# Four buffers in place of twenty for the normalised tiles of layer 0's router and scatter

## The chip, the cores and the metric

The kernel runs on one core of a Trainium2 chip. A core has five engines, each with its own queue that it works through in order: TensorE (PE in the profile; its weight loads are shown as PEld), VectorE (DVE), ScalarE (ACT), GpSimd (POOL) and SyncE (SP). Engines meet through semaphores: an instruction waits until another engine's, or a transfer's, count has been reached. The metric is device time in microseconds (us) of one execution, lower is better. Each run also shows the span from the program's first to its last instruction, and the TensorE clock that the chip granted (1.0 is full speed).

## What is computed

Four layers over x of 2 x 2048 tokens with 256 features in float32. Each layer normalises x and adds two branches to it. Only layer 0 matters here:

```python
xn = layernorm(x)                                   # 4096 tokens, 256 features
x = x + gated_linear_attention(xn) + experts(xn)    # layer 0

def experts(xn):                                    # 8 experts, the best 2 of each token
    w, idx = top_k(xn @ Wr, 2)
    comb = sum(softmax(w)[:, :, None] * one_hot(idx, 8), axis=1)
    h, g = xn @ W1[e], xn @ W3[e]                   # for each expert e
    y = (silu(h) * g) @ W2[e]
    return einsum('nec,ne->nc', y, comb)

def gated_linear_attention(x):                      # 4 heads, a state carried over the tokens
    q, k, v = x @ Wq / 8, x @ Wk, x @ Wv
    gk = log_sigmoid(x @ Wgk1 @ Wgk2 + bgk2) / 16
    S = S * exp(gk_t)[:, None] + k_t v_t^T;  o_t = q_t S      # for each token t
    return (rmsnorm(o) * g_norm_weight * silu(x @ Wg)) @ Wo
```

Layers 1 to 3 (a selective scan with a table of small experts, a retention layer, softmax attention of 16 heads with a second feed-forward branch) follow and are not touched. Layer 1 gathers rows of its tables with GpSimd's indirect DMAs, 512 of them at L805.

## The kernel before, in words

Tokens stand on the 128 partitions, so x is 32 tiles of 128 x 256, and stays in on-chip memory.

Layer 0 weaves three streams into one program: the attention of the two sequences (two chains of eight blocks of 256 tokens, the class `Attn0`) and the stream `moe`, which first routes and then runs 39 expert blocks of 256 token rows. The build then puts the woven instructions of each engine into an order of its own, by what they depend on and what it believes that they take; that order is fixed before the program runs. So an instruction of one stream can stand on a queue behind one of another.

The stream `route` does, in order:

- The routing loop: eight groups of four tiles. For each, statistics (L204 to L207), the four normalised tiles by `xnorm` (L195, on VectorE, from x, mean `mv` and scale `rs`), their transposes on TensorE (L212) and copies into `xT` (L213, ScalarE), the router's products (L68, tile `ps_e`), and the best eight of each token (L219, L220).
- Counting: which row of a buffer in HBM, `xgd`, each token takes for each of its two experts. Two matmuls count tokens (L242, L243), VectorE turns the counts into row numbers `pos` (L248 to L268).
- The scatter loop: for each of the 32 tiles, `xnorm` normalises it again, and two indirect DMAs issued by GpSimd (L273) write its 128 rows to their places in `xgd`, one for each of the two experts. The 64 scatters are declared free of order among themselves. The zero fill of `xgd` (L188, from SyncE's queue) comes before them.
- The numbers of the weight rows for each expert block (L283 to L288).

An expert block loads its weights `we` with an indirect DMA of GpSimd (L295), its 256 token rows `xg` with a DMA of SyncE (L300), transposes them on TensorE (L305), copies them on ScalarE (L306), and runs its products (L68, `ps_e`) with L315 to L317 between. The first load of `xg` waits for all 64 scatters.

An attention block projects to q, k, v and the gate (L68, `ps_g`; L388, L395, L399, L400, L403), computes the decay (L411 to L426: the scan `G`; L430 to L436: `qh`, `kh`), transposes `kh` on TensorE (L444), copies it on ScalarE (L446), makes the new states (L452 on TensorE, L461 on VectorE), then goes through seven levels of the intra-block products. A level is: the exponents E on VectorE (L476, L477), an exponential on ScalarE (L478), two products on VectorE (L481 `qt`, and L485; from the third block of a sequence on, L485 is GpSimd's), eight matmuls (L489), and two predicated copies on VectorE (L494). After the levels come the diagonal (L505 on TensorE, L510 on VectorE), the output products (L523, L527), their copy (L531), the norm (L538 to L543 `o`), transposes and the output projection (L549, L551, L68), and the addition to x (L554).

The tile `xn` is taken from a pool with a number of buffers, and both loops of `route` use the same ones in turn. A tile's L195 has to wait until the instructions that read the tile one round earlier are done: the transposes L212 in the routing loop, and the landing of both scatters in the scatter loop. The pool `wk` closes when `route` ends, and the pool of the expert blocks takes its place.

Of the kernel before, what the change touches and what calls it, by code (L numbers as in the profile page):

```python
# [14 lines left out]
F32 = mybir.dt.float32  # L15
# [8 lines left out]
P = 128  # L24
B, S, D = 2, 2048, 256
# [147 lines left out]
def route(g, tc, a, rt, wk, r, xgd):  # L173
# [17 lines left out]

    def xnorm(t):

        xn = wk.tile([P, D], F32, name="xn0", tag="xn0", bufs=20)
        nc.vector.tensor_scalar(xn, g.x[:, t, :], mv[:, t, 0:1], rs[:, t : t + 1], ALU.subtract, ALU.mult)  # L195
        return xn

# [2 lines left out]
    for n in (0, 4, 1, 5, 2, 6, 3, 7):  # L200
        t4 = slice(4 * n, 4 * n + 4)
        st = wk.tile([P, 4, 6], F32, name="st0", tag="st0", bufs=2)
        for i in range(4):
            nc.vector.bn_stats(st[:, i, :], g.x[:, 4 * n + i, :])  # L204
            nc.vector.bn_aggr(mv[:, 4 * n + i, :], st[:, i, :])
        nc.scalar.activation(rs[:, t4], mv[:, t4, 1], AF.Sqrt, bias=g.eps)
        nc.vector.reciprocal(rs[:, t4], rs[:, t4])  # L207
        xns = [xnorm(4 * n + i) for i in range(4)]
        for c in range(2):
            ps = g.psum()  # L210
            for i in range(4):
                nc.tensor.transpose(ps[:, i * P : (i + 1) * P], xns[i][:, c * P : (c + 1) * P], g.ident)  # L212
            nc.scalar.copy(g.xT[:, c, n * 512 : (n + 1) * 512], ps)  # L213
        ps = g.psum2()
        for i in range(4):
            mm(nc, ps[:, i * 8 : (i + 1) * 8],
               [(g.xT[:, k, (4 * n + i) * P : (4 * n + i + 1) * P], wr[:, k, :]) for k in range(2)])
        for i in range(4):
            nc.vector.max(top[:, 4 * n + i, :], ps[:, i * 8 : (i + 1) * 8])  # L219
            nc.vector.max_index(idx[:, 4 * n + i, :], top[:, 4 * n + i, :], ps[:, i * 8 : (i + 1) * 8])  # L220
        yield
# [48 lines left out]
    for t in [16 * b + n for n in range(NT // 2) for b in range(2)]:  # L270
        xn = xnorm(t)
        for j in range(2):
            ins = nc.gpsimd.indirect_dma_start(xgd, bass.IndirectOffsetOnAxis(ap=r.pos[:, j, t : t + 1], axis=0),  # L273
                                               xn, None)
            if t or j:
                tc.declare_no_dep(ins.ins, group="deal", reason="no two tokens share a row")
            tc.add_to_no_dep_group("deal", ins.ins)
        yield
        yield
# [1461 lines left out]
```

## Time and profile before

| what | us |
|---|---|
| median of 3 runs | 4375.13 |
| lowest and highest of them | 4360.28, 4397.19 |
| the profiled execution | 4351.19 |
| its span | 4349.4 |
| TensorE busy, share of the span | 3883.6, 89% |
| VectorE, ScalarE, GpSimd busy | 2536.0, 1980.0, 1302.8 |
| mean granted clock | 0.939 |

The stages, from the starts of their instructions: routing to 90 us, scatters (L273) 90.7 to 185.9 us, attention and experts to some 1200 us, then layer 1 to about 2385 us, and layers 2 and 3.

The additions of attention blocks to x (L554) start at 202, 261, 319, 377, 437, 500, 573 and so on to 1193 us. The transposes of the expert blocks (L305) start at 194, 253, 306, 368, 426, 461, 486 us for the first seven, with some 20 us from one to the next after that.

How the views are read. The page's first part gives the busy time of each engine, its second part the span in 40 slices of 109 us with the busy share in tenths. The waits name who waited for whom, with the total, the number and the longest of these waits; "remote" stands where a wait on a semaphore was ended by nothing that the profile shows, and "issue" where an engine was idle with nothing to wait for. In a timeline a row has the start, the duration, the engine, the line, the operation and the tiles that it writes and reads, and in square brackets the idle time ahead of it and what ended it. SPq and POOLq are the queues of those engines.

### The profile page before, as it was taken

Reading aid. Unit: us, or ns where it says so; the run is one execution under the profiler, and the core shown is the slowest. Engines: PE = TensorE matmul, PEld = TensorE weight load, DVE = VectorE, ACT = ScalarE, POOL = GpSimd, SP = SyncE. Lnnn points to the kernel's source line nnn. Section 1 sums busy time; section 2 is a strip of 40 time slices with the busy share of each in tenths; the row PEclk is TensorE's granted clock in tenths of the full one; section 3 lists DMA queues with packets and bytes.
Section 4 is the critical chain, followed back from the end, with each engine's and each line's share of the span. In section 5 each row is a group of like instructions: output and inputs, shape, how many; then the busy total and the mean of one; then the engine's idle time right before and its main releaser. Section 6 shows DMA issues by size and latency. Waiting matters only on the chain.

```text
span 4349.4 us, 58929 instructions
## 1 busy us (share of the span) xinstructions
PE 3883.6 (89%) x21524; PEld 2313.5 (53%) x21524; DVE 2536.0 (58%) x6438; ACT 1980.0 (46%) x3819; POOL 1302.8 (30%) x1307
## 2 busy tenths in 40 slices
PE   6388988999968898888885999999999999999999
PEld 5266666766745455455553777777433333333332
DVE  6254444454468898788888434434866655666560
ACT  3144343443345455445442332322555565566556
POOL 1402222222256665455556111112311111111201
PEclk7687999999989999999997999999999999999999
DMA  4200122222245665665568000000000000000000
GB/s 176 93 32 32 64 79 79 75 77 70 99 137 162 187 207 181 178 182 174 179 187 243 5 1 1 1 1 18 13 7 9 6 4 14 14 11 9 4 2 26
DMA packets 110947, 330.24 MB, mean 76 GB/s; under 512 B 30689, under 2 KB 63218, under 8 KB 104258
## 3 DMA queue, kind: packets, MB, share of 16 engines
q0 software_dynamic: 52720, 264.15, 19.6%
q1 hardware_dynamic: 55266, 59.22, 4.2%
q8 instruction: 170, 2.79, 0.3%
q10 hardware_dynamic: 2672, 3.10, 0.2%
q14 instruction: 119, 0.97, 0.1%
HBM read 286.69 MB, written 33.03 MB: 74 GB/s over the span
## 4 chain that ended last, share of the span: by engine, by line
PE 49%; DVE 4%; issue 2%; ACT 2%; POOL 1%; DMA 1%; another core or an unknown queue 1%; DVEq 0%; POOLq 0%; ACTq 0%
PE ps_e L1370 12%; PE ps_v L1433 6%; PE ps_a L68 6%; PE ps_f L68 6%; PE ps_m L68 4%; PE ps_c L68 3%; PE ps_k L68 2%; PE ps_m L1375 2%; PE ps_o L1059 1%; PE ps_m L1384 1%; PE ps_s L1370 1%; PE ps_h L839 1%; PE ps_s L1375 1%; DMA G<-in_tab_in,ind 1%
## 5 line engine op out<-in xcount | busy, mean ns | idle before, releaser
L1401 DVE TENSOR_REDUCE mp<-ps_m 128x1 f32<-128x512 f32 (+3 forms) x1120 | 628.1, 605 | 425.8 <-PE ps_e L1370 246.1
L1390 ACT ACTIVATE pt<-ps_e 128x512 f32<-128x512 f32 (+3 forms) x1120 | 537.2, 531 | 423.4 <-PE ps_e L1370 394.9
L1370 PE MATMUL ps_e<-qT,kT 32*128 32x512 f32 (+3 forms) x2240 | 627.8, 579 | 8.8 <-ACT pt L1390 8.8
L1375 PE MATMUL ps_m<-kT,qT 32*128 32x512 f32 (+3 forms) x2240 | 561.5, 576 | 1.1 <-DVE mp L1401 1.1
L1370 PEld LDWEIGHTS ps_e<-qT,kT 32*128 32x128 f32 x2240 | 211.0, 184 | 326.5 <-issue 116.6
L805 POOL DMA_INDIRECT G<-in_tab_in,ind x256 | 269.8, 1054 | 300.6 <-DVE ind L792 134.5
L1433 PE MATMUL ps_v<-pt,vals 128*32 128x512 f32 (+3 forms) x2560 | 307.5, 543 | 1.3 <-POOL pt L1394 0.6
L1394 POOL TENSOR_SCALAR_AFFINE_SELECT pt<-pt 128x256 f32<-128x256 f32 x256 | 104.4, 409 | 670.7 <-ACT pt L1390 670.4
L805 POOL DMA_INDIRECT G<-in_tab_out,ind x256 | 267.5, 1045 | 87.5 <-issue 58.1
L68 PE MATMUL ps_e<-xgT,we 128*128 128x256 f32 x936 | 241.6, 404 | 27.0 <-ACT xgT L306 17.2
L68 PE MATMUL ps_k<-wk,xt 128*128 128x512 f32 x512 | 263.1, 626 | 2.5 <-DVE ix L782 2.3
L68 PE MATMUL ps_f<-hb,l_b 128*128 128x512 f32 x1024 | 253.5, 400 | 0.0
L1050 DVE SCALAR_TENSOR_TENSOR hb<-ps_f,hb 128x512 fp32r<-128x512 f32 x128 | 86.7, 683 | 254.8 <-ACT hb L1049 253.5
L68 PEld LDWEIGHTS ps_e<-xgT,we 128*128 128x128 f32 x936 | 177.3, 198 | 70.6 <-ACT xgT L306 22.8
L68 PEld LDWEIGHTS ps_f<-hb,l_b 128*128 128x128 f32 x1024 | 190.1, 188 | 45.4 <-issue 7.7
L834 DVE CUSTOM_DVE_ANT_0 scr<-hid,G,gate 128x512 f32<-128x512 f32 x256 | 199.1, 778 | 19.9 <-ACT hid L821 7.3
L1375 PEld LDWEIGHTS ps_m<-kT,qT 32*128 32x128 f32 x2240 | 180.9, 184 | 25.6 <-issue 21.6
L494 DVE COPY_PREDICATED AT<-lm,ps_g 128x256 f32<-128x256 uint8 x224 | 104.8, 520 | 144.6 <-PE ps_g L489 141.3
L815 DVE CUSTOM_DVE_ANT_0 scr<-xn,G,gate 128x256 f32<-128x256 f32 x256 | 144.6, 565 | 45.3 <-DMA G<-in_tab_in,ind 42.1
L817 DVE SCALAR_TENSOR_TENSOR hid<-G,lin,hid 128x512 f32<-128x512 f32 x224 | 166.8, 745 | 2.4 <-DVE ix L782 0.4
L489 PE MATMUL ps_g<-qt,E 64*128 64x64 f32 x1792 | 138.7, 295 | 32.6 <-DVE E L485 23.9
L1049 ACT ACTIVATE hb<-ps_f 128x512 fp32r<-128x512 f32 x128 | 76.5, 597 | 200.5 <-PE ps_f L68 200.4
(426 smaller groups left out, 7667.6 us busy)
## 6 DMA issues: line engine op xcount, KB each, us to landing
xgd<-zero SPq DMA_DIRECT2D x13, 768.0 KB, 11.9
xg<-xgd SPq DMA_DIRECT2D x39, 256.0 KB, 2.9
yd<-ye SPq DMA_DIRECT2D x39, 256.0 KB, 3.1
G<-in_tab_in,ind POOLq DMA_INDIRECT x256
G<-in_tab_out,ind POOLq DMA_INDIRECT x256
kT<-qk SPq DMA_DIRECT2D x256, 16.0 KB, 1.8
out<-x SPq DMA_DIRECT2D x7, 512.0 KB, 3.3
x<-in_x ACTq DMA_DIRECT2D x4, 512.0 KB, 9.2
```

The source lines that it names most:

```text
L68: nc.tensor.matmul(out, lhsT, rhs, start=(i == 0), stop=(i == n - 1))
L489: nc.tensor.matmul(two[r][:, n * 64 : (n + 1) * 64], E[r * 64 : (r + 1) * 64, n * P : (n + 1) * P], qt[r * 64 : (r + 1) * 64, n * 64 : (n ...
L494: nc.vector.copy_predicated(AT[:, r].rearrange("p e (n t m) -> p e n t m", t=2, m=m)[:, :, :, 1, :], lm[:, li * 64 : (li + 1) * 64].unsque ...
L805: nc.gpsimd.indirect_dma_start(G, None, a[tab], bass.IndirectOffsetOnAxis(ap=k.ind[:, h, j : j + 1], axis=0))
L815: nc.vector.tensor_tensor_reduce(scr[:, 0:D], k.xn[:, j, :], G[:, 0:D], k.gate[:, h, j : j + 1], 0.0, ALU.mult, ALU.add, lin[:, h : h + 1])
L817: nc.vector.scalar_tensor_tensor(hs, G[:, D:768], lin[:, h : h + 1], hid if h == 0 else hs, ALU.mult, ALU.add)
L834: nc.vector.tensor_tensor_reduce(scr, hs, G[:, 0:512], k.gate[:, h, j : j + 1], 0.0, ALU.mult, ALU.add, lout[:, h : h + 1])
L1370: nc.tensor.matmul(te[i // step][:, i % step, c0:512], ge.kT[row(j), kt * P : (kt + 1) * P], ge.qT[row(j), qb * 512 + c0 : (qb + 1) * 512] ...
L1375: nc.tensor.matmul(tm[i // step][:, i % step, 0:w], gm.qT[row(j), qi * P : (qi + 1) * P], gm.kT[row(j), ch * 512 : ch * 512 + w], start=Tr ...
L1390: nc.scalar.activation(pt[:, o : o + step, c0:512], te[i // step][:, :, c0:512], AF.Exp, scale=0.25)
L1401: nc.vector.tensor_reduce(gm.mp[:, qi, j : j + step, ch], tm[i // step][:, :, 0:w], AX.X, ALU.max, negate=True)
L1433: nc.tensor.matmul(av[row(j), c0:512], vals[:, kt, at + 17 * j : at + 17 * j + 32], pts[j][:, c0:512], start=first, stop=last)
```

## The change

One number: the normalised tiles `xn` get four buffers in place of twenty.

```diff
     def xnorm(t):
 
-        xn = wk.tile([P, D], F32, name="xn0", tag="xn0", bufs=20)
+        xn = wk.tile([P, D], F32, name="xn0", tag="xn0", bufs=4)
         nc.vector.tensor_scalar(xn, g.x[:, t, :], mv[:, t, 0:1], rs[:, t : t + 1], ALU.subtract, ALU.mult)
         return xn
```

In the routing loop a group of four tiles now takes the buffers of the group before it. In the scatter loop a tile takes the buffer of the tile four places earlier, so that its L195 on VectorE waits for that tile's two scatters to land; before, it was the tile twenty places earlier. As the build orders by dependences, the instructions of the first part of layer 0 stand in another order on each engine than before. On TensorE's queue the first expert's transposes stand behind 290 matmuls of the attention blocks in place of 228; those of the second to sixth block behind 352, 420, 548, 608 and 736 in place of 352, 480, 608, 736 and 804; from the seventh (behind 856) on they stand at the same places. SyncE's order is the same.

## The prediction, made before the changed kernel was run

> **What bounds the kernel now.** I began with the page. TensorE is busy for 89% of the span and carries 49% of the chain of waits, so time is lost for good only where TensorE stands idle early. The slices show where: the second one (109 to 217 us) is the emptiest of the first half, 3 tenths on TensorE and 2 on VectorE. That is where GpSimd scatters (L273). The busy times by stretch sharpen it (columns: stretch, its length, then PE, PEld, DVE, ACT and POOL busy with their counts, granted clock, DMA share, GB/s):
>
> ```profile
> 104.00:127.00 23.00, 3.79 (x32) 3.52 (x32) 10.48 (x22) 5.20 (x7) 17.51 (x19) 0.50 0.27 97
> 127.00:151.00 24.00, 0.00 (x0) 0.00 (x0) 0.00 (x0) 0.60 (x1) 18.21 (x20) 0.50 0.29 104
> 151.00:170.00 19.00, 1.95 (x12) 1.55 (x14) 4.00 (x9) 1.48 (x3) 14.46 (x15) 0.50 0.29 104
> ...
> 218.00:486.00 268.00, 225.65 (x1316) 167.31 (x1314) 137.78 (x298) 108.68 (x229) 44.76 (x42) 0.83 0.10 33
> ```
>
> From 104 to 170 TensorE works 5.7 of 66 us, at a granted clock of 0.50, while GpSimd issues without a pause. So I asked the waits of VectorE, then those of ScalarE, between 85 and 195 us (columns: who for whom, us in total, times, longest), and VectorE's timeline:
>
> ```profile
> DVE AT L510 <- remote: 29.1, 2, 24.8
> DVE St L461 <- remote: 16.3, 1, 16.3
> DVE xn L195 <- DMA xgd<-xn,pos: 9.3, 6, 2.1
> ```
>
> ```profile
> ACT ks L446 <- issue: 40.9, 1, 40.9
> ```
>
> ```profile
> 107.20 0.41 DVE L195 TENSOR_SCALAR xn<-x,mv,rs 128x256 f32<-128x256 f32 x1 [1.42 <-DMA xgd<-xn,pos]
> 109.72 0.41 DVE L195 TENSOR_SCALAR xn<-x,mv,rs 128x256 f32<-128x256 f32 x1 [2.11 <-DMA xgd<-xn,pos]
> ...
> 151.72 0.72 DVE L510 COPY_PREDICATED AT<-lm,ps_g 128x512 f32<-128x512 uint8 x1 [24.78 <-remote]
> ```
>
> "Remote" means that nothing in the profile ended the wait. "Issue" is ScalarE idle with nothing to wait for. All three long ones (L510, L461, and L446 on ScalarE) read results of TensorE, whose rows say it was done: the matmuls L505 that L510 reads start at 118.34 and end at 120.39, and L510 starts 31 us later. Over the whole span VectorE has such waits of several us only here and in layer 1 (L778, 66.7 us in 13 waits), where GpSimd gathers by the same kind of DMA. So I read them as results of TensorE that become visible late while GpSimd issues indirect DMAs one behind the other; in the first 27 us of the scatters it did not happen. Last, GpSimd's own timeline: 62 scatters at 1.27 us each (0.96 busy, 0.30 between) from 90.70 to 169.72, then
>
> ```profile
> 168.76 0.96 POOL L273 DMA_INDIRECT xgd<-xn,pos  x1 [0.30 <-issue]
> 179.70 1.61 POOL L273 DMA_INDIRECT xgd<-xn,pos  x1 [9.98 <-DVE xn L195]
> ```
>
> because the last two tiles (179.03) stand on VectorE behind the stretch that waits for TensorE.
>
> **The change part by part.** No instruction is removed. Of the 32 tiles of the scatter loop, the last 12 waited for scatters before (a buffer of twenty back); now all but the first four do. In the routing loop each group of four tiles waits for the transposes of the group before.
>
> *Routing loop.* Seven groups get a wait. A group costs 8 matmuls of 1.04 us together, then four L195 of some 0.33 us from start to start, 1.4 us, which TensorE could stand idle for: seven times that is 10 us at most. But the router's and the first block's matmuls lie between the groups (31.1, 38.0, 44.0, 49.8, 67.4 us on TensorE's timeline), and TensorE afterwards waits 5.24 us for VectorE at L444 in any case. In the new order the counting matmuls L242 stand ahead of eight level matmuls and the next block's four projections, worth 2 us. I take 0, with -2 to +5 for the range.
>
> *The buffer cycle.* A scatter lands 2.5 us after its start: L195 at 109.72 was freed by the scatter of 107.21, and the one at 112.24 by that of 109.74. A tile's two scatters free its buffer 1.27 + 2.5 = 3.8 us after its first began; L195 takes 0.4. Four tiles last GpSimd 4 x 2.54 = 10.2 us. With VectorE at hand the cycle closes with 10.2 - 4.2 = 6 us to spare, so four buffers alone cost nothing. GpSimd stands only where VectorE has more than about 9 us of other work between two L195. And VectorE can no longer run ahead: it moves at 2.54 us a tile, and L400, L403, L411 and the copies L494 behind an L195 wait with it, then TensorE's next level (L489) for E and qt. That is hidden as long as VectorE has room: from 104 to 190 us it is busy for 26 of 86 us, the L195 among them. The zero-fill DMAs and the load of xg on SP's queue are not moved; xg still waits for the last scatter.
>
> *Gaps in the new order.* Between the 20th and 21st tile 24 instructions stand on VectorE, from L494 of the sixth level to the next block's E. The same piece in an undisturbed block runs from 230.43 to 242.4: 12 us, against a supply of 8.9 us (four tiles less the 1.2 us already spent), so a pause of 3.6 us. Between the 23rd and the 24th lie some 9 us (247.6 to 251.6 in the undisturbed block, and the 5.1 us wait before), against three tiles' supply of 7.6: 2 us. Together 6 us.
>
> *The sum.* The scatters' issue needs 79.0 + 2.5 = 81.5 us without pauses, 87.5 with: it ends at 90.7 + 87.5 = 178, where it ended at 185.9. Landing 2.5, the load of xg 6.2 (187.80 to 194.00), transposes and copy 1.8: the first expert could start at 189. The chain: VectorE reaches L543 of the first block near 168 (it was 186.3), L554 follows 7.9 us later (253.13 to 261.01 in the next block) at 176 (it was 202.4), and the first expert's products come 15.3 us after L554 (202.39 to 217.65), in both orders behind the second block's gate projection: 191 against 217.65. From there the order differs (experts two to six stand earlier) up to the seventh expert, which begins at 486 and is in the same place in both; TensorE is 84% busy in between and its instructions are the same, so I take what is won to stay. Gain 26 us with TensorE's results prompt. With them late, one or two waits last until GpSimd runs dry and some 6 us longer (GpSimd ended at 169.72, L461 got its result at 176.31): 6 to 12 us back. I take 18 us, nearer the undisturbed end, since GpSimd's pauses are just what lets such a wait end. The end of the gain: without any pause the first expert cannot start before 90.7 + 81.5 + 2.5 + 6.2 + 1.8 = 183, so 35 us.
>
> The profiled execution took 4351.19 (span 4349.4), so 4333 for it. The median of the runs lies 24 us above it (4375.13), so **4357**.
>
> Here a rule speaks against the change. The Trainium skill, SBUF — State Buffer, section "Who interferes with whom", has it that a DMA never contends with a compute engine. By it the late results would not come from the scatters, and holding these back would win nothing. The rows above disagree: 48 us of such waits on VectorE in 60 us of scatters, none in the 300 us behind them.
>
> **Rivals.** *Nothing is won.* GpSimd's queue already waits for the scatter eight back (22 short waits, 6.7 us), which is four tiles, so the limit is there already; and if the late results come from something else than the unbroken stream, VectorE loses the same 48 us. For it: L461 got its result 5 us late (L452 ended at 171.1, it started at 176.31) when GpSimd already stood. Time 4375, within 5 us.
>
> *Slower, by lockstep.* VectorE must wait for TensorE before a tile, GpSimd runs dry, and VectorE then waits for scatters: the two stand in turn. The new order has six places where work that reads TensorE's or ScalarE's results stands between tiles (before the 4th, 12th, 16th, 21st, 24th and 27th). Ten us of pause at each is 60 us: the issue ends at 232, the first expert starts at 232 + 10.5 = 243, 25 us late: 4400. It decides from 217.65 - 183 = 35 us of pauses on; a loss of 1% (44 us) needs 79 us, with results late by 10 us and more nearly everywhere. Against it: before 118 us nothing was late, under the same stream.
>
> *Much faster.* The plain runs lie between 9 and 46 us above the profiled one. If it is this stall that is longer in them, the change takes it away too: 18 + 24 to 18 + 46, so 42 to 64 us, around 4322.
>
> **How the numbers follow.** My forecast (a gain of 5 to 35 us, so 4340 to 4370) gets 46%, nothing won 18%, lockstep 18%, of which 10 beyond 1%, much faster 18%. A measurement of this kernel tells about 1% (44 us) from no change. So faster by more than that 18%, within it 46 + 18 + 8 = 72%, slower 10%. The range goes from the middle of the much faster case, 4322, to 20 us above the median, 4395, which holds part of lockstep and the routing loop's 5 us; outside are some 10% above and 8% below.
>
> **What would show it.** Right: the remote waits of L510 and L461 shrink to a few us or vanish; L195 waits for scatters some twenty times for about 2 us; GpSimd has a handful of pauses below 6 us before L273 and ends near 178; L554 first runs near 176, the first expert's products near 191, the seventh expert's transposes near 468. Wrong: waits of 15 us and more on TensorE's results in an interrupted stream; pauses before L273 over 35 us in sum; or the lead of the first expert lost by the seventh.

## The result, and the profile after

| | before | four buffers |
|---|---|---|
| median of 20 runs, us | 4375.5 | 4356.28 |
| lowest and highest | 4349.54, 4397.19 | 4338.6, 4394.95 |
| profiled execution, and its span | 4351.19, 4349.4 | 4342.98, 4341.2 |
| scatters (L273), first and last start | 90.7, 185.0 | 88.3, 191.5 |
| first L543, first L554 | 186.3, 202.4 | 171.4, 186.0 |
| first product of an expert | 217.6 | 207.9 |
| transposes (L305) of the seventh expert | 486.1 | 475.5 |
| the experts' results are first fetched, the last step of layer 0 (L167) | 1215.0 | 1195.5 |
| first unpacking of layer 2's weights on VectorE, taken as the end of layer 1 (L916) | 2384.0 | 2377.2 |

The ratio of the times is 0.9961, with a 95% interval of 0.9944 to 0.9978: 19 us between the medians, a gain that is clear of the noise, and below 1%. In the two profiled executions it is less: 19.5 us are won at L167, 6.8 are left at L916 and 8.2 at the end.

The same three stretches as before, in the kernel with four buffers (stretch, its length, then PE, PEld, DVE, ACT and POOL busy with their counts, granted clock, DMA share, GB/s):

```profile
104.00:127.00 23.00, 2.07 (x4) 1.16 (x4) 7.50 (x18) 1.23 (x2) 13.16 (x14) 0.52 0.21 74
127.00:151.00 24.00, 4.77 (x36) 4.23 (x36) 10.64 (x23) 5.81 (x7) 14.70 (x15) 0.50 0.25 88
151.00:170.00 19.00, 12.94 (x81) 10.72 (x80) 10.36 (x33) 9.17 (x26) 6.26 (x7) 0.50 0.12 42
```

TensorE now works 19.8 us of these 66 in place of 5.7, GpSimd 34 in place of 50. The stretch in which TensorE, VectorE and ScalarE stood still is split up, not gone. The waits of VectorE between 85 and 195 us (columns as before: who for whom, total, times, longest):

```profile
DVE xn L195 <- DMA xgd<-xn,pos: 23.6, 15, 2.7
...
DVE AT L494 <- remote: 10.2, 1, 10.2
DVE AT L510 <- remote: 7.7, 1, 7.7
```

and ScalarE's wait at L446, which was 40.9 us of "issue":

```profile
ACT ks L446 <- PE ps_g L444: 9.6, 1, 9.6
```

The longest wait on a result that was long done is 10.2 us in place of 24.8 on VectorE, and ScalarE's 40.9 us has become an ordinary wait for a matmul. (Of those 40.9 us, 14.3 were lateness itself: L444 ended at 154.2 and L446 started at 168.53. The rest stood behind VectorE's late L510, which L436 and L444 follow. So it is with VectorE's 16.3 us at L461: its matmuls L452 ended only at 171.1, 5.2 us ahead of it.)

The trace also keeps the moments at which a semaphore's count changes; the views do not print them. For the two L510 of the kernel before, TensorE's count rises at 151.70 and 157.30 us, where the rows let the matmuls end at 120.36 and 120.39; with four buffers at 148.64, where they end at 137.83. So it is the count itself that comes late, by 31 and 37 us before and 11 us now, and not VectorE that is slow to see it. (The ends of matmuls in the rows are modelled, so that the matmul itself was held up is not excluded.)

VectorE's and GpSimd's timelines show when the late results now come:

```profile
119.40 1.43 DVE L494 COPY_PREDICATED AT<-lm,ps_g 128x256 f32<-128x256 uint8 x2 [10.19 <-remote]
122.12 1.37 DVE L195 TENSOR_SCALAR xn<-x,mv,rs 128x256 f32<-128x256 f32 x4
...
148.66 0.72 DVE L510 COPY_PREDICATED AT<-lm,ps_g 128x512 f32<-128x512 uint8 x1 [7.71 <-remote]
...
164.34 0.44 DVE L494 COPY_PREDICATED AT<-lm,ps_g 128x256 f32<-128x256 uint8 x1 [6.41 <-PE ps_g L489]
```

```profile
115.74 0.96 POOL L273 DMA_INDIRECT xgd<-xn,pos  x1 [0.30 <-issue]
122.79 1.35 POOL L273 DMA_INDIRECT xgd<-xn,pos  x1 [6.09 <-DVE xn L195]
...
145.22 0.96 POOL L273 DMA_INDIRECT xgd<-xn,pos  x1 [0.30 <-issue]
157.23 0.95 POOL L273 DMA_INDIRECT xgd<-xn,pos  x1 [11.05 <-DVE xn L195]
...
169.47 0.95 POOL L273 DMA_INDIRECT xgd<-xn,pos  x1 [4.99 <-DVE xn L195]
```

VectorE stands at L494 for a matmul that ended at 100.7. It cannot refill buffers, so GpSimd issues its last scatter at 115.74 and stands. At 119.40, 3.7 us later, the result is there. The same again at L510: last scatter 145.22, result 148.66, 3.4 us. With twenty buffers GpSimd would have had work for another 50 us. The price is in the square brackets of GpSimd's rows: 22.1 us in three pauses, so that the scatters end 6.5 us later than before. The third, 5.0 us ahead of the scatter at 169.47, has no late result in it: VectorE waited 6.4 us for matmuls L489, which TensorE had only just done.

One trace is one execution. Layer 0 with four buffers was traced three times (here, and in gath_break and gb4 below, which differ in layer 1 alone): GpSimd pauses 22.1, 17.0 and 22.0 us, VectorE's longest wait on a late result is 10.2, 4.6 and 10.8 us, the first L554 comes at 186.0, 182.4 and 189.5, L167 at 1195.5, 1191.7 and 1193.4. Twenty buffers were traced twice (here and in gb20): 24.8 and 34.0 us, 202.4 and 198.7, 1215.0 and 1206.8. The lead at L167 is 11 to 23 us, whichever are compared.

### The profile page after: what moved, and what is told of

It is laid out like the page before. It is cut to its first block, busy times and chain, and to the rows that moved or that the text cites. A ratio compares the mean times of both kernels' runs of the same rounds, so it can differ in the third digit from the quotient of the medians.

```text
span 4341.2 us, 58946 instructions
## 1 busy us (share of the span) xinstructions
PE 3890.5 (90%) x21524; PEld 2316.4 (53%) x21524; DVE 2540.3 (59%) x6438; ACT 1976.5 (46%) x3817; POOL 1302.3 (30%) x1307
## 3 DMA queue, kind: packets, MB, share of 16 engines
q0 software_dynamic: 52720, 264.15, 19.5%
## 4 chain that ended last, share of the span: by engine, by line
PE 42%; DVE 4%; ACT 1%; POOL 1%; issue 1%; DMA 1%; another core or an unknown queue 0%; DVEq 0%; ACTq 0%; POOLq 0%
PE ps_e L1370 12%; PE ps_v L1433 6%; PE ps_a L68 6%; PE ps_f L68 6%; PE ps_m L68 4%; PE ps_m L1375 2%; PE ps_o L1059 1%; PE ps_m L1384 1%; PE ps_s L1370 1%; PE ps_s L1375 1%; DVE mp L1401 1%; DVE hid L817 1%; PE ps_x L68 0%; DVE scr L815 0%; DMA G<-in_tab_out,ind 0%
## 5 line engine op out<-in xcount | busy, mean ns | idle before, releaser
L805 POOL DMA_INDIRECT G<-in_tab_in,ind x256 | 270.3, 1056 | 299.4 <-DVE ind L792 133.8
L805 POOL DMA_INDIRECT G<-in_tab_out,ind x256 | 272.5, 1064 | 94.5 <-issue 56.9
L68 PE MATMUL ps_e<-xgT,we 128*128 128x256 f32 x936 | 237.2, 399 | 26.9 <-ACT xgT L306 16.5
L834 DVE CUSTOM_DVE_ANT_0 scr<-hid,G,gate 128x512 f32<-128x512 f32 x256 | 198.2, 774 | 20.9 <-DMA G<-in_tab_out,ind 8.3
L494 DVE COPY_PREDICATED AT<-lm,ps_g 128x256 f32<-128x256 uint8 x224 | 105.3, 521 | 167.7 <-PE ps_g L489 147.6
L68 PE MATMUL ps_c<-xs,l_wd 128*128 128x256 f32 x512 | 136.5, 422 | 34.8 <-ACT sp L691 20.1
```

The source lines that it names most:

```text
L68: nc.tensor.matmul(out, lhsT, rhs, start=(i == 0), stop=(i == n - 1))
L494: nc.vector.copy_predicated(AT[:, r].rearrange("p e (n t m) -> p e n t m", t=2, m=m)[:, :, :, 1, :], lm[:, li * 64 : (li + 1) * 64].unsque ...
L805: nc.gpsimd.indirect_dma_start(G, None, a[tab], bass.IndirectOffsetOnAxis(ap=k.ind[:, h, j : j + 1], axis=0))
L834: nc.vector.tensor_tensor_reduce(scr, hs, G[:, 0:512], k.gate[:, h, j : j + 1], 0.0, ALU.mult, ALU.add, lout[:, h : h + 1])
```

## Experiments

Theory A is the one of the prediction: an unbroken stream of scatters lets TensorE's results become visible late, and four buffers break it. Times are compared with runs of the kernel before on the same chip (median 4369.0 us in the first four runs, 4336.7 in the next four, on another chip, and 4374.2 in the last four, on a third). Diffs are against the kernel before.

**Which loop does it: split_scat4 and split_route4.** The two loops get buffers of their own; together no more than twenty fit.

```diff
-    def xnorm(t):
+    def xnorm(t, tag="xn0", bufs=16):
...
-        xn = wk.tile([P, D], F32, name="xn0", tag="xn0", bufs=20)
+        xn = wk.tile([P, D], F32, name="xn0", tag=tag, bufs=bufs)
...
-        xn = xnorm(t)
+        xn = xnorm(t, "xs0", 4)
```

For split_route4 the two numbers are 4 and 16.

> The scatter loop alone gets four buffers (a tag of its own); the routing loop keeps sixteen. Theory A (an unbroken stream of scatters keeps TensorE's results from becoming visible, four buffers tie the stream to VectorE and so break it): the whole effect of the change is here. Ratio 0.994 to 0.998; GpSimd stands behind VectorE's tiles for 15 to 25 us in 2 to 4 pauses before L273; remote waits of VectorE between 85 and 215 us sum to below 35 us, none above 12 us; L554 first runs at 184 to 190 us. Rival B (the gain comes from the routing loop's new order, which reached the row numbers L268 2.4 us earlier, or from the order behind it): little is left here, ratio 0.998 to 1.002, L554 at 195 to 203 us.

> The routing loop alone gets four buffers; the scatter loop has sixteen of its own (twenty would not fit beside them). Theory A: the stream runs unbroken until VectorE's last tiles, as before; a remote wait of 15 us or more is there between 85 and 215 us, their sum is 40 us or more, L554 first runs at 195 to 203 us, ratio 0.998 to 1.002 (0.9995 from the routing part's 2.4 us at best). Rival B: the gain is here, ratio 0.994 to 0.997 and L554 near 186 us.

split_scat4: median 4355.97 of 12 runs, ratio 0.9971 (0.9951 to 0.9991); L554 at 181.8, a little earlier than expected, two pauses of GpSimd, 17.3 us. One remote wait of VectorE was 13.1 us, a little more than expected; it ends at 196.6, behind the last scatter. split_route4: 4369.56, ratio 1.0004 (0.9985 to 1.0023), L554 at 207.5, later than either line had it. Its waits between 85 and 215 us, VectorE's and then ScalarE's:

```profile
DVE AT L510 <- remote: 23.1, 1, 23.1
```

```profile
ACT ks L446 <- remote: 41.3, 1, 41.3
```

Its scatters never stop (last start 171.7), and the long waits are those of before. (Of the 41.3 us, 22 are lateness: L444 ended at 157.8 and L446 started at 180.15.) So the scatter loop's buffers do it, and the routing loop gives nothing. The row numbers (L268) came at 90.2, 87.8, 88.7, 88.0 us in before, after and these two, but also at 84.6 in gb20 below, which has before's loops: the 2.4 us that the routing part seemed to win are within what one execution differs from another.

**Breaking the stream without tying it to VectorE: broken20.** GpSimd breaks the stream itself, at no wait of VectorE's.

```diff
-    rows = xgd.rearrange("(p q r) d -> p q (r d)", p=P, r=6)
+    rz = zero.rearrange("p (r d) -> p r d", r=6); rows = xgd.rearrange("(p q r) d -> p q (r d)", p=P, r=6)
...
-        xn = xnorm(t)
+        xn = xnorm(t); t in (2, 4, 6, 8, 10, 12, 14) and nc.gpsimd.tensor_tensor(rz, rz, xn.unsqueeze(1).to_broadcast([P, 6, D]), ALU.mult)
```

> Twenty buffers as before, VectorE free to run ahead, and GpSimd itself breaks the stream: before every fourth tile but the first it multiplies the tile of zeros by that tile (128x1536, an estimated 3.6 us from 2.36 us for 128x1024), seven breaks, 25 us in all. Theory A: results come through in the breaks; remote waits of VectorE between 85 and 215 us are 10 us at most each and below 35 us in sum; L554 first runs before 190 us although the scatters end some 10 to 15 us later than in the kernel before (near 197); ratio 0.994 to 0.999. Rival C (the late results have another cause than the unbroken stream): the waits stay at 48 us on VectorE and 41 us on ScalarE, L554 at 202 us or later, the scatters end 25 us later, ratio 1.000 to 1.006.

In the 85 to 215 us where before had 48 us of remote waits on VectorE, one is left:

```profile
DVE z L411 <- remote: 0.6, 1, 0.6
```

ScalarE has none, and its "issue" is 4.4 us at most. The same three stretches of broken20:

```profile
104.00:127.00 23.00, 6.90 (x49) 5.51 (x49) 21.46 (x39) 8.47 (x12) 19.60 (x14) 0.50 0.18 63
127.00:151.00 24.00, 16.75 (x88) 13.46 (x85) 11.94 (x32) 9.05 (x26) 20.28 (x16) 0.50 0.20 72
151.00:170.00 19.00, 18.53 (x112) 11.73 (x110) 6.86 (x14) 4.05 (x7) 15.47 (x14) 1.00 0.23 82
```

TensorE works 42 of 66 us, and L554 comes at 154.2, 48 us ahead of before, while 25 us of breaks are paid. For L510's matmuls, which end at 118.71 and 118.74, TensorE's count rises at 118.72 and 118.77. Seven pauses of 3.45 us give prompt results, at the same 64 scatters: what held them was the stream's being unbroken.

Two things changed along with the pauses. The build's order did: the first expert now stands where it stands with four buffers. But gb_brk below has the same places of the experts and waits of 20 us, so this order does not make results prompt. And the scatters are fewer per us on the whole; a slower stream without gaps was not tried.

Yet the time is 4366.56 (12 runs), ratio 0.998 (0.9954 to 1.0005), inside what was expected but little for 48 us. TensorE's timeline says where the lead stayed:

```profile
211.34 1.11 PE L305 MATMUL ps_e<-cst,xg 128*128 128x128 f32 x4 [41.80 <-DMA xg<-xgd]
```

The first expert's transposes stand on TensorE's queue ahead of most of the second block, and they wait for the last scatter (started 200.5). The second L554 comes at 254.2, only 7 us ahead of before. So there are two limits: results that come late, and the place of the first expert in TensorE's order against the end of the scatters.

**The floor: noscat.**

```diff
-        for j in range(2):
+        for j in range(2 if t == 0 else 0):
```

> Left out: all scatters but the first tile's two, so the experts compute on rows of zeros; everything else stays. Theory A: no wait on a result of TensorE above 3 us between 85 and 215 us, and L554 of the first block at 150 to 170 us (202.4 less the 48 us of remote waits, and a few more); the span loses 25 to 50 us. Rival C: the waits of L510, L461 and L446 stay, 20 us and more each, and L554 comes at 195 us or later.

No remote wait is left between 85 and 215 us; the waits of these two lines are now for matmuls that are running:

```profile
DVE AT L494 <- PE ps_g L489: 10.3, 4, 3.4
...
DVE St L461 <- PE ps_g L452: 2.0, 2, 1.2
```

L554 comes at 142.2 and the seventh expert begins at 425.4, so all that the scatters cost layer 0 up to there, the first expert's wait for them included, was 61 us. L554 lies 60 us ahead of before and so under the range expected, which had only VectorE's 48 us of remote waits in it; the other 12 were not traced. The median is 50 us under before, ratio 0.9869 (0.9833 to 0.9904); in the profile 22 us were left at the end.

**How long a break must be: broken20s.** As broken20, with `zero[:, 0:512]` and two repeats in place of six.

> As broken20 (twenty buffers, seven breaks by GpSimd), but each break is one operation on 128x512 in place of 128x1536: 1.3 us in place of 3.5, so that two scatters on either side of it start some 2.6 us apart, about the 2.5 us after which a scatter has landed. Theory A in its strict form (the scatters that are under way must drain, which took some 3.5 us after the last one's start in the changed kernel): the breaks are too short, a remote wait above 10 us is there between 85 and 215 us, L554 comes at 190 us or later. Theory A in its weak form (any gap in GpSimd's issue lets the results through): no remote wait above 3 us, L554 at 150 to 160 us as with the long breaks, and the scatters end near 186 us.

Between the two: the longest remote wait is 9.4 us, the six at L494 sum to 15.6; L554 at 159.0, scatters to 184.4. Neither the strict form (waits above 10 us, L554 at 190) nor the weak one (no wait above 3 us) holds: a gap of some 2.5 us between two starts lets some results through, one of 4.7 us let all through. One execution of 4334.8 us, beside a median of 4336.7, tells nothing of the time.

**Is it the index: plain20.**

```diff
-            ins = nc.gpsimd.indirect_dma_start(xgd, bass.IndirectOffsetOnAxis(ap=r.pos[:, j, t : t + 1], axis=0),
-                                               xn, None)
+            ins = nc.gpsimd.dma_start(xgd[(2 * t + j) * P : (2 * t + j + 1) * P, :], xn)
```

> Twenty buffers; the 64 scatters become 64 plain writes of the same 128 rows, issued by GpSimd at the same places but without indices, to rows that are fixed in advance (left out: the routing of the rows, so the experts compute on other tokens). If the late results come with indirect DMAs alone: no remote wait above 3 us between 85 and 215 us, L554 below 165 us. If any back-to-back stream of GpSimd's DMAs does it: waits of 15 us and more as in the kernel before, L554 at 190 us or later.

No remote wait, L554 at 146.8, as the first line said. But it does not settle it: a plain write takes GpSimd 0.54 us in place of 0.96, eight of them went ahead of the row numbers, and the stream of the other 56 was over after 33 us. In the kernel before nothing was late in the first 27 us either. Whether a plain stream of 80 us would hold results stays open. Its one execution took 4273.28 us, 63 us under the median of before on the same chip (4336.7); L167 is at 1155.9, where noscat, almost without scatters, has 1150.9.

**More buffers than four: bufs8.**

```diff
-        xn = wk.tile([P, D], F32, name="xn0", tag="xn0", bufs=20)
+        xn = wk.tile([P, D], F32, name="xn0", tag="xn0", bufs=8)
```

> Eight buffers in both loops: VectorE may be seven tiles (17.8 us of scatters) ahead. Theory A: the stream breaks only where VectorE has more than some 17 us of other work or waits between two tiles, so it breaks less often than with four (three pauses, 22.1 us) and each late result lasts until GpSimd has used up its tiles: one or two remote waits of 12 to 20 us on VectorE, 1 or 2 pauses of GpSimd, L554 between 186 and 200 us, ratio 0.996 to 1.000. Rival B (the order, which is nearly that of four buffers): L554 at 186 us and ratio as with four, 0.994 to 0.998.

4324.83 (10 runs), ratio 0.9977 (0.9956 to 0.9998). L554 at 188.7, two pauses (13.3 and 4.2 us), as theory A had it, but no single wait of 12 to 20 us: VectorE's are 8.1 at most. The wait of an engine is not the whole lateness, though. L510's matmuls ended at 131.8 and L510 started at 155.1, 23 us later, between before's 31 and the 11 with four buffers; VectorE had other work in between and stood in three parts (7.0, 4.9 and 8.1 us). ScalarE's long "issue" waits (11.8 at L416, 9.1 at L428, 15.5 at L435) are no late results: each ends within 0.1 us after the instruction that it reads from. TensorE's order is nearly that of four buffers, but the intervals of the two overlap, so the ratio does not tell A from B.

**The same thing in layer 1: gath_break.** GpSimd gathers there 512 times (L805), in streams that are nearly all of 14 or fewer. This kernel has four buffers, and:

```diff
-            G = wk.tile([P, 768], F32, name="G1", tag="G1", bufs=NG)
+            G = wk.tile([P, 768], F32, name="G1", tag="G1", bufs=NG); h in (4,) and nc.gpsimd.tensor_tensor(G.rearrange("p (r d) -> p r d", r=3), xj.unsqueeze(1).to_broadcast([P, 3, D]), xj.unsqueeze(1).to_broadcast([P, 3, D]), ALU.mult)
```

> The changed kernel (four buffers), and in layer 1 the same idea applied to GpSimd's gathers (L805): ahead of the fifth of every eight gathers GpSimd computes a product of 128x768 into the buffer that is gathered into next (an estimated 1.8 us from 2.36 us for 128x1024; 64 times, 115 us of GpSimd's time). Theory A: late results are what costs layer 1 its remote waits too (in the changed kernel between 1230 and 2380 us: la L690 83.2 us, mx L778 56.9, xr L665 25.2), and they fall by at least half; layer 1 (L167 to L916, 1182 us in the changed kernel) gets 20 to 60 us shorter, ratio to the kernel before 0.980 to 0.992. Rival: the waits stay within 30 us of what they were, or GpSimd's own time takes the place of what is won: ratio 0.994 to 1.010.

The waits of layer 1 (1230 to 2380 us) in the kernel with four buffers:

```profile
ACT la L690 <- remote: 83.2, 14, 11.8
...
DVE mx L778 <- remote: 56.9, 10, 8.9
...
ACT xr L665 <- remote: 25.2, 6, 7.5
```

and in gath_break all that there is, with one of the breaks in GpSimd's timeline:

```profile
ACT xr L665 <- remote: 0.7, 1, 0.7
```

```profile
1993.42 1.41 POOL L805 DMA_INDIRECT G<-in_tab_out,ind  x1 [0.30 <-DVE lin L815]
1994.85 1.47 POOL L804 TENSOR_TENSOR G<-x 128x768 f32<-128x768 f32 x1
1996.60 1.15 POOL L805 DMA_INDIRECT G<-in_tab_out,ind  x1 [0.27 <-POOL G L804]
```

64 breaks of 1.48 us (the estimate was 1.8) took nearly all of 171 us of such waits away; with the same breaks gb4, gb20 and gb_brk below have 11.8, 10.0 and 0.6 us left. L167 to L916 took 1138 us, in the kernel with four buffers 1182; on the same chip plain20, bufs8 and broken20s, without these breaks, had 1149, 1148 and 1170. So the gain in layer 1 is 10 to 44 us by what it is held against, and much of the 171 must have lain beside other work. What is clear is the spread: L167 to L916 takes 1138 to 1143 us in all four traces with breaks, and 1148 to 1212 in the ten without. Median 4302.49 (4 runs), ratio 0.9907 (0.9891 to 0.9924): inside what theory A expected.

**The change again, with layer 1 quiet: gb20 and gb4.** Both have layer 1's breaks as above; gb20 has twenty buffers, gb4 four.

> The kernel before (twenty buffers) with the breaks of gath_break in layer 1's gathers alone. gath_break took layer 1's remote waits from 171 us to below 1 us, so with the same breaks on both sides the change of buffers can be measured without them. If the lead of layer 0 is real and was blurred by layer 1: this kernel lies 13 to 22 us above gb4 (run beside it), the difference of the two leads at L167 in the profiles being 15 to 25 us and kept to the end within 3 us; ratio to the kernel before 0.992 to 0.997. Rival (layer 1 takes the lead back for another reason than its late results): the two lie within 8 us, although their L167 differ by 15 us or more.

> The same kernel as gath_break (four buffers, breaks in layer 1's gathers), run again beside gb20. Ratio to the kernel before 0.989 to 0.992; L167 15 to 25 us ahead of gb20's; 13 to 22 us below gb20 at the end. By the rival within 8 us of gb20.

gb20: 4319.36 (6 runs, 4314.59 to 4327.7), ratio 0.9873 (0.9851 to 0.9894). gb4: 4303.41 (5 runs, 4296.31 to 4309.91), ratio 0.9835 (0.981 to 0.9859). Their ranges do not meet, and the medians are 16 us apart, as the lead had it. At L167 it is 13.4 us (a little less than expected), at L916 16.5, at the end 18.7: what layer 0 wins is kept (it grew by 5 us, where 3 were allowed). Both lie further under the kernel before than expected, since the breaks are worth 55 us here (gb20), against 34 between before and gath_break (with four buffers' share in it) on the other chip. Twenty buffers with a quiet layer 1 still have the old stall:

```profile
DVE AT L510 <- issue: 34.0, 1, 34.0
```

**Fewer and shorter breaks in place of four buffers: gb_brk.** gb20, and in the scatter loop broken20s' break ahead of t = 3, 6, 9 and 12 only.

> Twenty buffers, layer 1's breaks, and in layer 0 four short breaks by GpSimd itself (128x512, 1.3 us, ahead of every twelfth scatter from the thirteenth on), some 6 us in all where four buffers cost the scatters 22 us. If two things bound layer 0's start (TensorE's results, and the end of the scatters, behind which the first expert stands): the scatters end near 180 us (191.5 with four buffers), L554 comes by 180, the first expert's transposes L305 at 190 to 196 (206.5 with four), L167 is 0 to 10 us ahead of gb4's, and the time lies 0 to 10 us below gb4's. If the breaks are too few: one remote wait above 15 us is left, L554 at 190 us or later, and the time lies above gb4's.

4302.9 (5 runs), ratio 0.982 (0.9794 to 0.9845): level with gb4. The scatters end at 179.8 as expected, but the breaks are too few: waits of 20.2 us (L494) and 16.4 (ScalarE's L551), L554 at 191.0, L305 at 206.3 in place of 190 to 196. What GpSimd saves, the late results take; the time, though, is not above gb4's, as that line of the expectation had it.

**The tightest tie: split_scat2.** split_scat4 with 2 in place of 4.

> Two buffers in the scatter loop (sixteen of their own in the routing loop): the tie between VectorE and GpSimd at its tightest. A tile's scatters take 2.54 us, its buffer is free 3.8 us after they began and refilled 0.4 us later, so two buffers still close the cycle with 0.9 us to spare; VectorE may be one tile (2.5 us) ahead. Theory A: more and shorter breaks, no remote wait above 8 us; but GpSimd now stands in every gap of VectorE's above 3 us, 30 to 50 us of pauses in sum, the scatters end at 200 to 220 us and the first expert's L305 follows 15 us behind: L305 at 215 to 235, ratio 0.998 to 1.004. If pauses cost nothing and only the late results count: L305 below 210 and a ratio below 0.997.

The steps came as expected, and the time did not: 4329.86 (4 runs), ratio 0.9895 (0.9866 to 0.9924), 44 us under before. One step was off as well: ScalarE has a remote wait of 10.2 us (L388), where none above 8 was expected. VectorE's largest remote waits by line, then GpSimd's pauses, then the first two L554 and the first expert:

```profile
DVE AT L494 <- remote: 5.6, 2, 3.0
```

```profile
POOL xgd L273 <- DVE xn L195: 35.9, 6, 10.7
```

```profile
159.64 0.69 DVE L554 TENSOR_TENSOR x<-x,ps_g 128x512 f32<-128x512 f32 x1 [4.75 <-remote]
230.00 0.69 DVE L554 TENSOR_TENSOR x<-x,ps_g 128x512 f32<-128x512 f32 x1 [8.65 <-PE ps_g L68]
```

```profile
221.52 1.11 PE L305 MATMUL ps_e<-cst,xg 128*128 128x128 f32 x4 [5.93 <-DMA xg<-xgd]
```

GpSimd pauses 35.9 us, the scatters end at 209.5, the first expert starts at 221.5, and still the second L554 comes 31 us ahead of before and the seventh expert begins at 449.7 in place of 486.1. TensorE's order fits this. The trace has 380 matmul rows of attention blocks ahead of the first expert's transposes before, 500 with four buffers and in broken20, and 620 here (some matmuls have two rows): the build put the expert further back in the second block's work. So TensorE does that work while the scatters end, and waits 5.9 us for `xg` where broken20 waits 41.8. This run changed the tie and the order together; a kernel with the late place alone was not tried, nor split_scat2 with layer 1's breaks, which would be the next to run.

## Why the prediction was right, and where it was not

The time (4357 against a median of 4356.28) and the size of the gain, below 1%, were right, and so was the mechanism. That the number came within 1 us is luck: some of its steps were far off and made up for each other, and for the profiled execution, which it put at 4333, the time was 4342.98.

- *Late results come from the unbroken stream.* Shown: noscat has no remote wait, broken20 with all 64 scatters none above 0.6 us, split_route4 the long ones of before. By the rule of the Trainium skill that spoke against it (SBUF — State Buffer, "Who interferes with whom") VectorE's long waits would have stayed in noscat; the measurements decide against it as a guide to this case. The rule is about ports of on-chip memory, and no run here shows where the results are held, only that they are.
- *Routing loop, 0.* Right: split_route4 at 1.0004 (0.9985 to 1.0023).
- *The buffer cycle costs nothing by itself.* Right: 15 waits of L195, 2.7 us at most, and GpSimd stands only where VectorE has a longer wait.
- *Issue without pauses, 81.5 us.* 82.0 with four buffers. It was added up from 62 scatters until 169.72; the trace has 60, so that by its own rows the sum was 84.1.
- *Pauses of GpSimd, 6 us.* This term was mis-sized: 22.1 us. The two pauses that it had, ahead of the 21st and the 24th tile, are 11.1 and 5.0 us in place of 3.6 and 2; 7.7 us of the first are a late result, which the undisturbed block could not show. The third, 6.1 us ahead of the 12th tile, was not in the sum; it stands behind the late L494 of 10.2 us. The issue therefore ended at 192 (88.3 + 81.5 + 22.1) in place of 178. That is the lockstep rival's mechanism, at 22 us instead of 60.
- *L543 near 168, and late results 6 to 12 us back.* L543 came at 171.4, though late results had cost VectorE 18 us in two turns by then. Both sizes were off, and they cancelled: with prompt results broken20 reaches L543 at 144.0, so 168 was some 24 us too late for prompt results, and the lateness that four buffers leave costs some 27 us up to there (estimates from the two traces).
- *From L543 to the first expert, 7.9 and 15.3 us.* They took 14.6 and 21.9. The first expert's products came at 207.9 in place of 191. Late results are in both: the count that L554 waits for rises at 185.95 where its matmuls end at 182.29, and L494 waits 9.3 us until 198.2. The granted clock is in both, too: 0.50 from 172.8 to 178.3 us and from 190.9 to 199.5, where the pieces that the prediction measured by had 0.92 and 1.00.
- *What is won stays.* The lead was 16.4 us at the first L554, 9.0 at the second, 10.6 at the seventh expert (18 were predicted there), and 19.1 at the last. The prediction held that place and lead were settled once the seventh expert stood alike in both orders; the lead still grew, and why stays open. In the pair of profiles layer 1 then took 12 us of it back; with layer 1 quiet (gb20 and gb4) it was kept. 18 us at the end was right with a path that was not.
- *Nothing won*: out, by the interval. *Much faster*, from a longer stall in plain runs: out. gb20 has the stall in full (34.0 us), and its six runs lie at 4314.59 to 4327.7 with the profiled one, 4318.46, among them; the kernel before lies at 4365.62 to 4389.63 beside it. So most of that spread goes with layer 1's gathers. *Lockstep*: it was to decide from 35 us of pauses on. split_scat2 paused 35.9 and was faster all the same. The bound took the first expert's place in TensorE's order as given, and there it stands later.

What the runs do not separate is the order. Every kernel that broke the stream and became faster also got another order on TensorE's queue, so how much of the 16 to 19 us comes from earlier results and how much from the new places of the experts stays open. broken20 has both, and won no clear time, with its scatters ending 9 us later than with four buffers. noscat and plain20 have before's places of the experts (376 rows ahead of the first, in place of 380) and prompt results, and lie 50 and 63 us under before; but in noscat the first expert waits for two scatters alone, and in plain20 the last one starts at 125.7 us.

## What to carry to other kernels

Before costing a wait as "one more dependence", look for an engine that works without a pause while others stand on results that are long done: there a wait, or an operation of 1.3 to 1.5 us every eight or twelve DMAs (gath_break, gb_brk), can win time. Give the tie to the loop that issues the DMAs, and check in the new order what stands behind the last of them: 48 us of lead shrank to 7 at one early instruction on TensorE's queue. And when one stage of a kernel makes its runs differ by tens of us, quiet that stage first on both sides, and small changes elsewhere can be measured.

## What the hardware showed that was not expected

- With twenty buffers, a result of TensorE stayed unseen the longer, the longer the stream and the shorter its breaks, in one trace each: VectorE's longest wait is 0.6 us with 8 scatters and gaps of 4.7 us (start to start), 9.4 with 8 and gaps of 2.5 us, 20.2 with 12 and 2.5 us, and 23.1, 24.8 and 34.0 in three kernels without breaks. With four buffers two came 3.7 and 3.4 us after the last scatter before a pause had started; elsewhere they came up to 8.4 us after it (L510 at 180.05 in split_route4), and several amid a stream (L510 at 151.72 in the kernel before, L494 at 151.35 in gb_brk). What lets them through stays open.
- Gathers of 128 rows of 3 KB do the same within streams of mostly 14: waits of up to 11.8 us, nearly all gone with a break of 1.48 us in eight.
- A low clock goes with the stall: from 151 to 170 us the granted TensorE clock was 0.50 in before and after and 1.00 in broken20, where TensorE had worked 16.75 of the 24 us ahead of that (0.00 in before, 4.77 after). That this work alone decides is not shown: gb_brk had 10.82 us of it, and 0.50 too.
